# 72 direct columns in bf16 parts instead of 48 in f32, their sums added later, and comparisons that start later in a group

## The chip, the core and the metric

The kernel runs on one core of a Trainium2 chip. The core has a matmul engine (PE; its weight loads are listed as PEld), a vector engine (DVE), a scalar engine (ACT), a general engine (POOL) and a queue that issues transfers (SP). Each works through its own instructions in order, and they wait for one another by semaphores. The metric is device time in microseconds (us), the median of several executions; lower is better. A profile is one further execution, taken with the hardware profiler.

## What is computed

A graph layer on N = 6250 nodes and E = 206250 edges, 128 features each, all in f32:

```
edge_aggr = zeros(N, 128).at[src].add(edge_attr)
combined  = concat([x, edge_aggr, global_feat repeated], -1) @ W_c + b_c
h = softplus(combined @ W1 + b1)
h = softplus(h @ W2 + b2)
out = layernorm(x + h @ W3 + b3)
```

The edges are sorted by the other end (`dst`), so `src`, by which rows of `edge_attr` are summed, is in no order. This sum, over 206250 rows of 512 bytes, is nearly all of the work.

## The kernel before

**Edges as columns.** Edge e of the first 206208 lies on partition e // 1611 and in column e % 1611; the last 42 make one more column. A column is thus 128 edges, one on each partition. The 1612 columns are dealt with in two ways.

**Direct columns.** The first 48 are summed straight into the table of node sums, `sums_t` (features on partitions, 25 blocks of 256 nodes along the free axis). The nodes are cut into 13 windows of 512 (`WIDE`; the last holds 256). For a column and a window ACT makes a 128x512 table of ones and zeros, `hot`: one operation gives |node - position|, a second, over the two columns of a `QUAD` at once, gives max(0, 1 - that). PE multiplies the column's 128 rows (stationary, 128x128) with it and adds over the 12 columns of a `SET` in one PSUM tile, `direct_sum`, of which there are two. DVE then adds the tile to `sums_t`. The function `direct_steps` makes these steps: `begin` (node numbers, and for all windows the difference `less` that ACT uses as bias), `load` of the first set's rows, and one step per job (set, window, two columns). In step i ACT compares for job i (`compare`) and PE multiplies for job i - 2 (`add`). Where the sixth job of a window is done, the same `add` has DVE do the addition (L598). `hot` has three buffers, a set's rows two.

**Scattered columns.** The other 1564 are cut into 11 groups, given by `GROUPS` as (columns, sub). Within a group the rows are sorted by block of 256 nodes: `positions` counts and scans (DVE, PE) to find each edge's place. SP loads ten columns at a time (`load_rows`), POOL writes each row's code (`code_rows`, L639) and then sends each column's 128 rows to their places in one of three DRAM areas by an indirect DMA (`scatter_rows`, L647). `fill_rows` has set the area's unused places to -1 before. `reduce_steps` takes the group back in chunk loads of 1024 rows in block order: `load` (SP), `match` (L428, DVE: is the row's code equal to the position?, 128x2048; or the same by two kinds of ACT operations, L423 and L425), `product` (L442, PE, 16 instructions a load) and `add` (L459, DVE, one 128x256 addition per run of one block into `sums_t` at an offset read at run time). There are five chunk buffers, three of `hot` and three of the PSUM tile `part`.

**Which engine compares.** `TAIL` names, for the last groups, a share: every share-th chunk load is compared on DVE, the others on ACT. With (2, 4, 4) the last three groups have ACT on 1/2, 3/4 and 3/4 of their loads; all earlier groups are on DVE alone.

**The order.** The order of PE, DVE, ACT and SP is the order of the Python code. The main loop goes through the groups g, and in each through its tens of columns. Each ten loads rows three tens ahead (`LEAD`), scatters its own, and then issues a share of four lists: `prep` (positions of the next group), `sums` (the reduction of group g - 1, spread so that it ends at 95% of the group), `other` (node rows for the layers behind, in groups 3 to 5) and `filled`. To these come direct steps, spread over groups 1 to 6 in proportion to `left`, an estimate of each group's spare columns. The shares of one ten are interleaved evenly. `sums` begins with three chunk loads; of a group of 24 tens the first ten issues two steps, the second two more.

All transfers of SP are issued in one fixed order (`put_dma`), so a row load stands behind every chunk load ahead of it. After the last group its reduction is done alone, and the dense layers follow, in node tiles of 512.

Of the kernel before, what the change touches and what calls it, by code (L numbers as in the profile page):

```python
# [7 lines left out]
F32 = mybir.dt.float32  # L8
# [8 lines left out]
P = 128  # L17
# [5 lines left out]
GROUPS = ((40, 1), (120, 2), (200, 4), (240, 4), (240, 4), (240, 4), (226, 4), (130, 2), (72, 2),  # L23
# [4 lines left out]
TAIL = (2, 4, 4)  # L28
# [3 lines left out]
DIRECT = 48  # L32
SET = 12
WIDE = 512
QUAD = 2
FILL = 4
# [15 lines left out]
def kernel(  # L52
# [119 lines left out]
    with ExitStack() as phase:  # L172
# [377 lines left out]
        def direct_steps():  # L550


            steps = []
# [3 lines left out]
            less = keep.tile([P, NW, ND], F32, name="less")  # L557
            rows_in, hot_of, sum_of = {}, {}, {}

            def begin():  # L560

                first = keep.tile([P, NW], F32, name="first")
                nc.gpsimd.iota(first, pattern=[[WIDE, NW]], base=0, channel_multiplier=0,
                               allow_small_or_imprecise_dtypes=True)
                part, node, _ = whole_nodes(0, ND)
                nc.vector.tensor_copy(node, part)
                nc.vector.tensor_tensor(
                    less, node.unsqueeze(1).to_broadcast([P, NW, ND]),
                    first.unsqueeze(2).to_broadcast([P, NW, ND]), op=ALU.subtract)
# [6 lines left out]

            def compare(c, w, q):
                n = min(WIDE, NB * BL - w * WIDE)
                hot = direct_p.tile([P, QUAD, WIDE], F32, name="direct_hot", bufs=3)
                hot_of[c, w, q] = hot  # L580
                for j in range(QUAD):
                    nc.scalar.activation(hot[:, j, :n], iota_f[:, :n], AF.Abs,  # L582
                                         bias=less[:, w, c + q + j:c + q + j + 1], scale=-1.0)
                nc.scalar.activation(hot[:, :, :n], hot[:, :, :n], AF.Relu, bias=ones[:, :1],  # L584
                                     scale=-1.0)

            def add(c, w, q):
                n = min(WIDE, NB * BL - w * WIDE)
                k = min(SET, ND - c)
                hot = hot_of.pop((c, w, q))  # L590
                if q == 0:
                    sum_of[c, w] = ps.tile([P, WIDE], F32, name="direct_sum", bufs=2)
                for j in range(QUAD):
                    nc.tensor.matmul(sum_of[c, w][:, :n], rows_in[c][:, q + j, :], hot[:, j, :n],  # L594
                                     start=(q + j == 0), stop=(q + j == k - 1))
                if q + QUAD == k:
                    here = sums_t[:, w * WIDE:w * WIDE + n]
                    nc.vector.tensor_add(here, here, sum_of.pop((c, w))[:, :n])  # L598
# [3 lines left out]
            steps += [begin, lambda: load(0)]  # L602
            for i in range(len(jobs) + 2):
                def one(i=i):
                    if i < len(jobs):
                        c, w, q = jobs[i]
                        if (w, q) == (NW // 2, 0) and c + SET < ND:
                            load(c + SET)
                        compare(*jobs[i])
                    if i > 1:  # L610
                        add(*jobs[i - 2])
                steps.append(one)
# [42 lines left out]
        with tc.manual_schedule(engines={ET.PE, ET.DVE, ET.Activation, ET.SP}):  # L655
# [36 lines left out]
            for g in range(1, G - 4):  # L692
                left[g] = max(0.0, groups[g][1] - groups[g][0]
                              - groups[g - 1][3] * groups[g - 1][2] / 3 - (9 if 3 <= g < 6 else 0))
            direct_at = 0.0
# [3 lines left out]
            for g in range(G):  # L699
# [13 lines left out]
                for q in mine:  # L713
                    load_rows(i + LEAD)
# [5 lines left out]
                    for w, todo in enumerate((prep, sums, other, filled)):  # L720
                        share = (q - mine[0] + 1) / len(mine)
                        if w == 2:
# [182 lines left out]
```

## Time and profile before

| | us |
|---|---|
| median of 14 runs (2926.16 to 2974.1) | 2953.72 |
| profiled execution, its time | 2927.22 |
| its span, first to last instruction | 2925.3 |
| busy: PE, DVE, ACT, POOL | 1933.8, 1353.3, 891.4, 1588.0 |
| mean granted PE clock, as a share | 0.821 |

The scatters of the eleven groups begin at 26, 84, 266, 637, 1057, 1486, 1897, 2300, 2529, 2673 and 2739 us, and the last ends at 2778. What follows is the end of the reduction, to about 2850, and the layers.

In the profile a line such as L428 is a line of the kernel's file. A group is all instructions of one line, engine and operation: how many, their busy time, the mean of one in ns, the idle time of the engine just before them and what ended most of it. The ends of matmuls are modelled: of matmuls in a row the distance between starts tells the rate, not the duration. "Remote", or "another core or an unknown queue", is a wait whose end the profile can't put down to an instruction. The chain is the work that ended last, followed back from the end; only work on it, or work that would come onto it, moves the time.

### The profile page before, as it was taken

The page shows a single profiled execution, that of the slowest core. Times are in us where ns is not written, and L with a number is a line of the kernel's source. Part 1 is how long each engine was busy: PE and PEld are TensorE (multiplying, and loading weights), DVE is VectorE, ACT ScalarE, POOL GpSimd, SP SyncE. Part 2 cuts the span into 40 slices and gives each one's busy share as a digit, 9 for nine tenths or more (in the row PEclk, how much of TensorE's full clock was granted, in tenths as well). Part 3 has the DMA queues.
Part 4 walks back from the last instruction along what each step waited for, and adds up shares of the span by engine and source line. Part 5 has one row for each costly group of instructions (what it writes and reads, how often), then busy time and mean ns, then how long its engine had stood idle before and what let it go on. Part 6 is the DMA issues. An engine that isn't in the chain of part 4 may idle for free.

```text
span 2925.3 us, 21792 instructions
## 1 busy us (share of the span) xinstructions
PE 1933.8 (66%) x6470; PEld 1266.8 (43%) x6470; DVE 1353.3 (46%) x1976; ACT 891.4 (30%) x1186; POOL 1588.0 (54%) x1782
## 2 busy tenths in 40 slices
PE   2326387645887855768756777727877658747786
PEld 0113134422454532545433554524555446635663
DVE  5224344511544423554424554416554347647576
ACT  0223273423532413333214223204323200000586
POOL 5756446465456555555564655564555645554406
PEclk7557698776988977889878988868988879878898
DMA  9959347553454642556453445533545446645632
GB/s 286 260 156 253 92 135 212 154 160 93 136 175 148 182 131 82 152 139 174 132 155 95 142 131 155 146 93 104 156 133 154 139 123 195 187 118 158 169 88 88
DMA packets 418892, 437.18 MB, mean 149 GB/s; under 512 B 37807, under 2 KB 308774, under 8 KB 418774
## 3 DMA queue, kind: packets, MB, share of 16 engines
q1 hardware_dynamic: 368582, 332.43, 41.6%
q0 software_dynamic: 50048, 103.35, 10.8%
q8 instruction: 51, 0.84, 0.1%
q14 instruction: 67, 0.55, 0.1%
q10 hardware_dynamic: 144, 0.02, 0.0%
HBM read 262.62 MB, written 173.03 MB: 149 GB/s over the span
## 4 chain that ended last, share of the span: by engine, by line
PE 39%; another core or an unknown queue 28%; DVE 16%; issue 11%; ACT 4%; DVEq 1%; DMA 0%; ACTq 0%
PE part L442 26%; PE direct_sum L594 11%; DVE hot L428 5%; DVE sums_t L459 4%; ACT direct_hot L582 2%; DVE so_far L320 1%; ACT direct_hot L584 1%; DVE pos L354 1%; DVE sums_t L598 1%; DVE at L352 1%; DVE ib L266 1%; DVEq L453 1%; PE small L343 0%; ACT hot L423 0%
## 5 line engine op out<-in xcount | busy, mean ns | idle before, releaser
L647 POOL DMA_INDIRECT place<-rows,pos x1564 | 1505.6, 963 | 1231.0 <-DMA rows<-in_edge_attr 576.8
L442 PE MATMUL part<-hot,chunks 128*128 128x256 f32 x4524 | 1196.3, 421 | 667.0 <-DVE hot L428 342.1
L442 PEld LDWEIGHTS part<-hot,chunks 128*128 128x128 f32 x4524 | 941.1, 212 | 952.1 <-DVE hot L428 394.6
L582 ACT ACTIVATE direct_hot<-iota_f,less 128x512 f32<-128x512 f32 (+1 forms) x624 | 405.1, 696 | 1615.6 <-remote 703.5
L594 PE MATMUL direct_sum<-direct_hot,direct_rows 128*128 128x512 f32 (+1 forms) x1248 | 601.2, 612 | 135.1 <-ACT direct_hot L584 68.1
L428 DVE SCALAR_TENSOR_TENSOR hot<-chunks,iota_ps 128x2048 f32<-128x2048 f32 (+1 forms) x266 | 602.8, 2267 | 0.0
L459 DVE TENSOR_TENSOR sums_t<-sums_t,part 128x256 f32 x808 | 338.8, 419 | 462.8 <-remote 321.4
L594 PEld LDWEIGHTS direct_sum<-direct_hot,direct_rows 128*128 128x128 f32 x1248 | 244.0, 200 | 365.9 <-issue 267.1
L584 ACT ACTIVATE direct_hot<-direct_hot,ones 128x1024 f32<-128x1024 f32 (+1 forms) x312 | 348.6, 1117 | 10.2
L598 DVE TENSOR_TENSOR sums_t<-sums_t,direct_sum 128x512 f32<-128x512 f32 (+1 forms) x52 | 34.7, 667 | 628.9 <-remote 285.8
L423 ACT ACTIVATE hot<-iota_f,chunks 128x256 f32<-128x256 f32 x146 | 60.4, 497 | 374.8 <-PE part L442 357.8
L352 DVE TENSOR_TENSOR at<-small,ib 128x500 f32<-128x500 f32 (+3 forms) x80 | 52.9, 662 | 91.3 <-remote 71.6
L354 DVE TENSOR_REDUCE pos<-at 128x20 int32<-128x500 f32 (+3 forms) x80 | 86.9, 1086 | 2.7
L320 DVE TENSOR_TENSOR_SCAN so_far<-iota_ps,ib 128x1500 bf16<-128x1500 f32 (+7 forms) x30 | 85.9, 2863 | 0.0
L338 PE MATMUL small<-ib,upto_h 128*128 128x500 bf16 (+3 forms) x80 | 33.3, 417 | 67.5 <-DVE at L352 42.3
L533 DVE COPY x_t<-small 128x512 f32<-128x512 f32 (+1 forms) x13 | 8.6, 658 | 148.2 <-remote 115.8
L853 POOL TENSOR_TENSOR x_sb<-x_sb,b_all 128x512 f32<-128x512 f32 (+1 forms) x13 | 15.3, 1220 | 78.7 <-DMA x_sb<-in_x 78.7
L541 DVE TENSOR_SCALAR z_x<-small,z_bias 128x512 f32<-128x512 f32 (+1 forms) x13 | 9.3, 718 | 87.3 <-remote 39.9
L339 PE MATMUL small<-so_far,ones_h 128*128 128x500 bf16 (+3 forms) x80 | 33.7, 421 | 21.9 <-issue 11.4
L339 PEld LDWEIGHTS <-ones_h 128*128 128x128 bf16 x80 | 8.2, 103 | 90.4 <-issue 89.0
L266 DVE TENSOR_TENSOR ib<-block,iota_ps 128x1500 bf16<-128x1500 bf16 (+7 forms) x30 | 44.3, 1505 | 0.0
L277 PE MATMUL small<-ib,ones_h 128*128 128x500 bf16 (+3 forms) x80 | 24.2, 412 | 29.4 <-DVE ib L266 16.3
(117 smaller groups left out, 533.3 us busy)
## 6 DMA issues: line engine op xcount, KB each, us to landing
chunks<-place SPq DMA_DIRECT2D x281, 516.0 KB
rows<-in_edge_attr SPq DMA_DIRECT2D x154, 640.0 KB
place<-fill SPq DMA_DIRECT2D x252, 258.0 KB
place<-rows,pos POOLq DMA_INDIRECT x1564
x_sb<-in_x SPq DMA_DIRECT2D x24, 256.0 KB
direct_rows<-in_edge_attr SPq DMA_DIRECT2D x4, 768.0 KB
out<-y SPq DMA_DIRECT2D x12, 256.0 KB
src_i<-in_src SPq DMA_DIRECT2D x1, 761.5 KB
```

The lines of the kernel that those rows point to most:

```text
L266: nc.vector.tensor_tensor(ib, block[:, a:b].unsqueeze(1).to_broadcast([P, NB, n]), iota_ps[:, :NB].unsqueeze(2).to_broadcast([P, NB, n]), ...
L320: nc.vector.tensor_tensor_scan(t, iota_ps[:, 1:2].to_broadcast([P, NB * n]), in_block[k][0], 0.0, op0=ALU.mult, op1=ALU.add)
L352: nc.vector.tensor_mul(at, got.pop((k, j0)), in_block[k][1][:, :, j0:j1])
L354: nc.vector.tensor_reduce(pos[:, a - c0 + j0:a - c0 + j1], at.rearrange("p b g -> p g b"), axis=mybir.AxisListType.X, op=ALU.add)
L428: nc.vector.scalar_tensor_tensor(hot[:, :m], chunks[i][:, :m, D:W].to_broadcast([P, m, BL]), code_of(g), iota_ps.unsqueeze(1).to_broadcast ...
L442: nc.tensor.matmul(part[:, s - q, :], t[:, s * sub + j, :D], hot[:, s * sub + j], start=(j == 0), stop=(j == sub - 1))
L459: nc.vector.tensor_add(here, here, part[:, s - q, :])
L582: nc.scalar.activation(hot[:, j, :n], iota_f[:, :n], AF.Abs, bias=less[:, w, c + q + j:c + q + j + 1], scale=-1.0)
L584: nc.scalar.activation(hot[:, :, :n], hot[:, :, :n], AF.Relu, bias=ones[:, :1], scale=-1.0)
L594: nc.tensor.matmul(sum_of[c, w][:, :n], rows_in[c][:, q + j, :], hot[:, j, :n], start=(q + j == 0), stop=(q + j == k - 1))
L598: nc.vector.tensor_add(here, here, sum_of.pop((c, w))[:, :n])
L647: s = nc.gpsimd.indirect_dma_start(out=dst, out_offset=bass.IndirectOffsetOnAxis(ap=at, axis=0), in_=rows[:r, j, :], in_offset=None)
```

## The change

- `DIRECT` goes from 48 to 72, and the seventh entry of `GROUPS` from 226 to 202 columns: 24 columns move from the scattered to the direct ones. The direct sets go from four to six.
- The direct product is made in bf16. A new step, `split`, cuts each set's f32 rows on DVE into three bf16 parts that add up to the f32 value: the upper half of its bits, the upper half of what is left (written back into the lower half of the row's own place), and the rest (`direct_low`). PE multiplies each of the three with `hot`, now bf16, and adds them in the same f32 PSUM tile. `less` is made per set instead of once.
- The addition of a finished window to `sums_t` moves out of `add` into `total`, which is issued three steps later, at the head of a step.
- The first direct step is now the load of the first rows, and is issued in the last ten of group 0.
- In groups of more than eight tens the first ten issues the first three steps of `sums` (the chunk loads), and the later tens' shares are counted from the second ten on.
- `TAIL` has a fourth entry and other shares: group 7 and group 8 have ACT on half of their loads, the last two groups on all. `iota_f` grows to four blocks with it.

```diff
-GROUPS = ((40, 1), (120, 2), (200, 4), (240, 4), (240, 4), (240, 4), (226, 4), (130, 2), (72, 2),
+GROUPS = ((40, 1), (120, 2), (200, 4), (240, 4), (240, 4), (240, 4), (202, 4), (130, 2), (72, 2),
           (38, 1), (18, 1))
-TAIL = (2, 4, 4)
+TAIL = (2, 2, 100, 100)
-DIRECT = 48
+DIRECT = 72
+SPLIT = 2
...
-            less = keep.tile([P, NW, ND], F32, name="less")
-            rows_in, hot_of, sum_of = {}, {}, {}
+            node_f = keep.tile([P, ND], F32, name="node_f")
+            first = keep.tile([P, NW], F32, name="first")
+            less_of = {}
+            rows_in, low_in, hot_of, sum_of = {}, {}, {}, {}
...
+            def halves(t):
+                return [t.bitcast(BF16).rearrange("p c (d h) -> p c d h", h=2)[:, :, :, h]
+                        for h in (0, 1)]
+            def split(c):
+                n = min(SET, ND - c)
+                less = less_of[c] = direct_p.tile([P, NW, SET], F32, name="less", bufs=2)
+                nc.vector.tensor_tensor(
+                    less[:, :, :n], node_f[:, c:c + n].unsqueeze(1).to_broadcast([P, NW, n]),
+                    first.unsqueeze(2).to_broadcast([P, NW, n]), op=ALU.subtract)
+                low_in[c] = direct_p.tile([P, SET, D], BF16, name="direct_low", bufs=2)
+                for a in range(0, min(SET, ND - c), SPLIT):
+                    b = min(a + SPLIT, SET, ND - c)
+                    rest = direct_p.tile([P, SPLIT, D], F32, name="direct_rest")[:, :b - a]
+                    x_c = rows_in[c][:, a:b]
+                    nc.vector.tensor_sub(rest, x_c, halves(x_c)[1])
+                    nc.vector.tensor_sub(low_in[c][:, a:b], rest, halves(rest)[1])
+                    nc.vector.tensor_copy(halves(x_c)[0], halves(rest)[1])
...
-                hot = direct_p.tile([P, QUAD, WIDE], F32, name="direct_hot", bufs=3)
+                hot = direct_p.tile([P, QUAD, WIDE], BF16, name="direct_hot", bufs=3)
...
-                for j in range(QUAD):
-                    nc.tensor.matmul(sum_of[c, w][:, :n], rows_in[c][:, q + j, :], hot[:, j, :n],
-                                     start=(q + j == 0), stop=(q + j == k - 1))
+                for j in range(q, q + QUAD):
+                    addends = halves(rows_in[c][:, j:j + 1]) + [low_in[c][:, j:j + 1]]
+                    for i, part in enumerate(addends):
+                        nc.tensor.matmul(sum_of[c, w][:, :n], part[:, 0], hot[:, j - q, :n],
+                                         start=(j == 0 and i == 0), stop=(j == k - 1 and i == 2))
                 if q + QUAD == k:
-                    here = sums_t[:, w * WIDE:w * WIDE + n]
-                    nc.vector.tensor_add(here, here, sum_of.pop((c, w))[:, :n])
+                    ready.append((c, w, n))
+            def total():
+                c, w, n = ready.pop(0)
+                here = sums_t[:, w * WIDE:w * WIDE + n]
+                nc.vector.tensor_add(here, here, sum_of.pop((c, w))[:, :n])
...
-            steps += [begin, lambda: load(0)]
-            for i in range(len(jobs) + 2):
+            steps += [lambda: load(0), begin, lambda: split(0)]
+            ready, behind = [], []
+            for i in range(len(jobs) + 6):
                 def one(i=i):
+                    if behind and behind[0] <= i:
+                        behind.pop(0)
+                        total()
                     if i < len(jobs):
                         c, w, q = jobs[i]
                         if (w, q) == (NW // 2, 0) and c + SET < ND:
                             load(c + SET)
+                        if (w, q) == (NW - 2, 0) and c + SET < ND:
+                            split(c + SET)
                         compare(*jobs[i])
-                    if i > 1:
+                    if 1 < i < len(jobs) + 2:
                         add(*jobs[i - 2])
+                        if len(ready) > len(behind):
+                            behind.append(i + 3)
...
+            direct_first = direct[:1]
+            direct = direct[1:]
...
+                    if g == 0 and q == mine[-1]:
+                        for step in direct_first:
+                            step()
                     load_rows(i + LEAD)
...
                         share = (q - mine[0] + 1) / len(mine)
+                        if w == 1 and len(mine) > 8:
+                            if q == mine[0]:
+                                now.append(todo[:3])
+                                done[w] = 3
+                                continue
+                            share = (q - mine[0]) / (len(mine) - 1)
```

More of the change, by code (lines that the diff above doesn't have):

```diff
@@ L556, in direct_steps @@
             NW = -(-NB * BL // WIDE)
-            less = keep.tile([P, NW, ND], F32, name="less")
-            rows_in, hot_of, sum_of = {}, {}, {}
+            node_f = keep.tile([P, ND], F32, name="node_f")
+            first = keep.tile([P, NW], F32, name="first")
+            less_of = {}
+            rows_in, low_in, hot_of, sum_of = {}, {}, {}, {}
             def begin():
-                first = keep.tile([P, NW], F32, name="first")
                 nc.gpsimd.iota(first, pattern=[[WIDE, NW]], base=0, channel_multiplier=0,
                                allow_small_or_imprecise_dtypes=True)
[L565 to L569, printed above, removed]
+                part, _, _ = whole_nodes(0, ND)
+                nc.vector.tensor_copy(node_f, part)
             def load(c):
@@ L582, in compare @@
                     nc.scalar.activation(hot[:, j, :n], iota_f[:, :n], AF.Abs,
-                                         bias=less[:, w, c + q + j:c + q + j + 1], scale=-1.0)
+                                         bias=less_of[c][:, w, q + j:q + j + 1], scale=-1.0)
                 nc.scalar.activation(hot[:, :, :n], hot[:, :, :n], AF.Relu, bias=ones[:, :1],
```

## The prediction

> **What bounds the kernel now.** I read the busy shares first (PE 66%, POOL 54%, DVE 46%, ACT 30%: nothing is full), then the chain that ended last, the groups, the stretches of single groups, and the timeline where the chain waits. The chain, by engine and by line:
>
> ```profile
> PE 39%; another core or an unknown queue 28%; DVE 16%; issue 11%; ACT 4%; DVEq 1%; DMA 0%; ACTq 0%
> PE part L442 26%; PE direct_sum L594 11%; DVE hot L428 5%; DVE sums_t L459 4%; ACT direct_hot L582 2%; DVE so_far L320 1%; ACT direct_hot L584 1%; DVE pos L354 1%; DVE sums_t L598 1%; DVE at L352 1%; DVE ib L266 1%; DVEq L453 1%; PE small L343 0%; ACT hot L423 0%
> ```
>
> POOL, whose 1564 scatters are the largest group, is not on it. The groups of lines (busy time, mean of one, idle time before and what ended it) say why:
>
> ```profile
> L647 POOL DMA_INDIRECT place<-rows,pos x1564 | 1505.6, 963 | 1231.0 <-DMA rows<-in_edge_attr 576.8
> L582 ACT ACTIVATE direct_hot<-iota_f,less 128x512 f32<-128x512 f32 (+1 forms) x624 | 405.1, 696 | 1615.6 <-remote 703.5
> L594 PE MATMUL direct_sum<-direct_hot,direct_rows 128*128 128x512 f32 (+1 forms) x1248 | 601.2, 612 | 135.1 <-ACT direct_hot L584 68.1
> L584 ACT ACTIVATE direct_hot<-direct_hot,ones 128x1024 f32<-128x1024 f32 (+1 forms) x312 | 348.6, 1117 | 10.2
> L598 DVE TENSOR_TENSOR sums_t<-sums_t,direct_sum 128x512 f32<-128x512 f32 (+1 forms) x52 | 34.7, 667 | 628.9 <-remote 285.8
> ```
>
> POOL stands 577 us for rows that SP has not yet asked for: SP issues rows and chunks in one order, and stands for chunk buffers that PE must free. So PE with DVE and ACT sets the pace. Two stretches (second and fourth group's scatters; columns PE, PEld, DVE, ACT, POOL busy, granted clock):
>
> ```profile
> 265.70:636.70 371.00, 230.94 (x683) 129.69 (x682) 148.30 (x213) 154.83 (x198) 196.25 (x220) 0.82 0.56 155
> 1057.30:1486.20 428.90, 298.26 (x975) 197.26 (x974) 183.15 (x214) 126.07 (x156) 235.95 (x265) 0.82 0.47 135
> ```
>
> In the later one PE is busy 298 of 429 us, POOL's 240 scatters at 1.27 us would take 304. The rest is waiting. Two kinds stand in the timeline. First, work of PE that is over by its record is seen by others much later, while POOL scatters without a gap:
>
> ```profile
> 1919.07 0.60 PE L531 MATMUL small<-ident,x_sb 128*128 128x128 f32 x4
> 1936.56 0.96 POOL L647 DMA_INDIRECT place<-rows,pos  x1 [0.30 <-issue]
> 1964.44 0.69 DVE L533 COPY x_t<-small 128x512 f32<-128x512 f32 x1 [51.60 <-remote]
> ```
>
> There is one core, so "another core or an unknown queue" is this kind. Second, DVE stands in `direct_steps`' addition (L598) for a matmul issued in the same step, comes late to the next comparison (L428), and PE stands for that:
>
> ```profile
> 2174.54 1.88 PE L594 MATMUL direct_sum<-direct_hot,direct_rows 128*128 128x512 f32 x4
> 2176.26 0.93 PE L277 MATMUL small<-ib,ones_h 128*128 128x500 bf16 x4
> 2176.46 0.69 DVE L598 TENSOR_TENSOR sums_t<-sums_t,direct_sum 128x512 f32<-128x512 f32 x1 [9.47 <-PE direct_sum L594]
> 2177.06 2.28 DVE L428 SCALAR_TENSOR_TENSOR hot<-chunks,iota_ps 128x2048 f32<-128x2048 f32 x1
> 2179.40 3.72 PE L442 MATMUL part<-hot,chunks 128*128 128x256 f32 x16 [2.21 <-DVE hot L428]
> ```
>
> **The change, part by part**, against the profiled execution (2927.2 us, span 2925.3); the runs' median is 0.9% above it.
>
> *Direct matmuls.* One f32 product is two instructions (1248 for 48 columns x 26 halves of 13 windows). Four of 512 elements start within 1.88-0.59 = 1.29 us: 0.43 each. Of four bf16 ones of 500 the first starts at 2176.26, the third at 2176.69: 0.215 each. Before: 1152 x 0.43 + 96 narrow x 0.215 = 516 us. After: 72 x 3 products in 12 wide windows and a narrow one, 2592 x 0.215 + 216 x 0.11 = 581. That is +65, and at the granted 0.82 +79. On the path all of it, or 11% of the span out of 601 us busy (0.53), which gives 42: between them **+60**. The weight loads (103 ns for contiguous bf16 in the by-shape groups, 190 for f32) are shorter than a matmul, strided halves included unless they exceed f32's.
>
> *Direct comparisons.* 312 pairs become 468: 754 us of ACT become 1131, +377. The `hot` tile in bf16 has no row here; nearest is the same operation in f32, so no gain is taken. The Trainium skill, "ScalarE: Activation LUTs", section "What ACT_TABLE_LOAD costs", says one element a cycle for f32 and bf16 alike, which speaks against hoping for more; by it the term stays as it is, while at twice the speed it would be 565 us of ACT and -22 here. No run here shows a bf16 one yet. On the path: 3% of the span out of 754 us (0.12), **+44**. Ends: 0 where ACT stays hidden; 137 where the first two groups go by ACT. The schedule puts 66 and 97 pairs on their 12 and 20 tens of columns (43 and 63 before): 5.5 x 2.41 = 13.3 us per ten against 12.7 of scattering. 57 added pairs x 2.41 = 137.
>
> *Splitting on DVE.* Per two columns two subtractions and a copy of 256 elements; nearest rows of 240 take 0.41, 0.41, 0.28. 36 x 1.10 = 40, six smaller `less` against one of 0.81, +1; 26 more additions, +17. 58 us, of which DVE's share on the chain (468 of 1353, 0.35) gives **+20**; ends 0 and 58. Each split is 19 operations, about 7 us in one piece; behind it stand the comparisons, and PE for them. Its own reader comes 12 pairs later. In the trace a two-input subtraction-like row (L203, 0.41 us, at 737.74) stands beside scatters at 737.39 and 738.65, 1.26 apart as always. The Trainium skill, "SBUF — State Buffer", section "Who interferes with whom", would have such an operation shut out a GpSimd one that reads SBUF; by that rule POOL would lose up to 40 us, by the row nothing, and the row is taken.
>
> *Later additions.* `total` runs three steps after the last matmul, so DVE no longer drains PE. What goes is the pause behind it, 0.69 + 2.28 less what PE still holds; 2.21 is seen, 52 x 2.2 = 114. What is late next is L459, which lets DVE lead PE by two chunk loads only, and in the "unknown" waits needs the same late news of PE. So **-80**; ends 0 and -171 (half of the 342 us, 236.0 and 106.2, that the waits of L598 show for PE and issue rather than "remote").
>
> *24 columns fewer to scatter.* 24 x 1.27 = 30 us of POOL, not on the chain. Reduction: L442, L428 and L459 have 35% of the span, 1024/1564 x 24 = 16; the unknown waits scale with scatters, 819/1564 x 24 = 13. **-29**; ends -10, -46 (both and POOL's own).
>
> *The last groups' comparisons.* ACT alone for the last two. A pure ACT load takes 3.30 + 2.00 less overlap = 5.24 us; from 2784 to 2849 the 14 loads took 4.6 each: +9. Half of group 7's 23 comparisons leave DVE (4.1 us a load with additions) for a stage paced by PE's 3.5: -7 at best, little under its waits. **+8**; ends -7, +16.
>
> *Group starts.* The code sets `done` to 3 and then back: in groups 1 to 6 the second ten's share rounds to 1 or 2 of the steps. So nothing is compared there, one or two loads are issued a second time (8 in all; the instruction list of SP has 290 chunk loads, 282 wanted), and comparisons begin with the third ten in groups of 24 tens, not the second (with the second in group 7 alone). On SP three chunk loads, which wait for the last group's scatters, now stand together ahead of the next rows; each repeat takes one of five chunk buffers and 516 KB. Direct work fills the time. **+6**; ends -40 (DVE no longer stands for the first chunk) and +40 (8 x 5 us). The first `direct_rows` load moves ahead of two row loads on SP, before the first group's end: 0, three tens of rows are already there; ends -15 (the wait it had) and +3.
>
> Sum: 60 + 44 + 20 - 80 - 29 + 8 + 6 = **+29**, 2956; times 2953.72/2927.22 = 1.009: **2983 us**, 1% slower.
>
> **Rivals.** *The additions give more* (faster). For it: 629 us of DVE standing, PE's 342 us for comparisons. Against: 286 of the 629 are "remote", which a deferral by 7 us does not outlast. At -171 the sum is -62: 2865, times 1.009 **2891**. It decides once PE's wait for L428 falls by more than 125 us.
> *ACT becomes the bound early.* For it 13.3 against 12.7 us, and ACT's 703 us of late news. Against: those stretches took 15.2 and 18.6 us per ten anyway. With 137 for 44: 3049, **3077**.
> *It cancels*: additions near -110; 2926, **2953**.
> *The change does not do what it says*: the start of the comparisons is shifted by another ten and repeats loads, as worked out; alone +-40, within the cases above.
>
> **How the numbers follow.** Forecast (slower by 0.5 to 2.5%) 0.38, additions 0.34, ACT 0.15, cancelling 0.13; so slower 0.53, same 0.13, faster 0.34. 0.5%, 15 us, is about what a measurement of this kernel can tell from no change. Distances to the ends, added as squares, make 124 us; 8 in 10 about 100 either side: **2885 to 3080**. The forecast's own range is 2968 to 3028.
>
> **What would show it.** L594's successor: 2808 matmuls, 0.215 apart at full clock, near 600 us of work. ACT direct near 1130 us, its bf16 form at 0.71. The addition's idle time far below 629, PE's wait for comparisons below 342 by some 80. Scatter waits for rows about as before: if they fall by over 100 us, the rival of the additions holds. If the stretch of the first two groups grows by 100, ACT's does. 290 chunk loads. I am wrong if the "unknown" 28% moves by itself: I scale it by scatters, yet nothing in the trace says what starts it.

## The result, and the profile after

The changed kernel takes 3057.35 us (median of 10 runs, 3030.7 to 3072.44) against 2957.06 us before: a ratio of 1.0356, 95% interval 1.0322 to 1.039. It is slower by 3.6%, where I had forecast 1%. The ratio, here and below, is that of the fast runs of both kernels alone and so can lie a little off the quotient of the medians, here 1.034. The chain that ended last, by engine and by line, after the change:

```profile
PE 41%; another core or an unknown queue 26%; ACT 16%; issue 12%; DVE 5%; DVEq 0%; ACTq 0%
PE part L444 26%; PE direct_sum L620 12%; ACT direct_hot L606 7%; ACT direct_hot L608 6%; DVE hot L430 2%; ACT hot L425 1%; DVE sums_t L461 1%; PE small L345 1%; PE small L340 0%; PE small L341 0%; PE small L342 0%; ACT away L828 0%; ACT away L823 0%; ACT away L822 0%
```

DVE has largely left the chain (16% to 5%) and ACT has come onto it (4% to 16%); PE grew by 2 points of a longer span, and the unknown part stayed at 0.8 ms. The groups (busy, mean of one in ns, idle time before and what ended most of it); L687, L606, L608, L620 and L628 are what L647, L582, L584, L594 and L598 were, and L444, L430 and L461 are L442, L428 and L459:

```profile
L687 POOL DMA_INDIRECT place<-rows,pos x1540 | 1478.9, 960 | 1382.6 <-DMA rows<-in_edge_attr 705.6
...
L606 ACT ACTIVATE direct_hot<-iota_f,less 128x512 bf16<-128x512 f32 (+1 forms) x936 | 604.8, 693 | 1375.5 <-remote 965.3
...
L620 PE MATMUL direct_sum<-direct_hot,direct_rows 128*128 128x512 bf16 (+1 forms) x1872 | 598.6, 402 | 443.2 <-issue 242.8
...
L608 ACT ACTIVATE direct_hot<-direct_hot,ones 128x1024 bf16<-128x1024 bf16 (+1 forms) x468 | 521.9, 1115 | 15.2
...
L628 DVE TENSOR_TENSOR sums_t<-sums_t,direct_sum 128x512 f32<-128x512 f32 (+1 forms) x78 | 51.9, 666 | 371.0 <-remote 197.8
```

The addition's idle time fell from 629 to 371 us, but ACT now stands 965 us for "remote" (703 before) and POOL 706 us for rows (577). The stages of the scatters of groups 2 and 4, counted from 0 (the same two, with the same columns, as in the prediction):

```profile
285.40:701.50 416.10, 267.19 (x1074) 142.45 (x1073) 167.77 (x259) 252.69 (x322) 195.84 (x220) 0.82 0.50 141
1148.80:1611.00 462.20, 319.30 (x1277) 199.46 (x1278) 197.65 (x245) 202.21 (x256) 235.53 (x264) 0.84 0.44 128
```

They were 371 and 429 us long. The scatters of groups 1 to 7 now begin at 84, 285, 702, 1149, 1611, 2061 and 2434 us. So groups 1 to 5, which hold most of the direct work, are 164 us longer, and group 6 is 30 us shorter, for its 24 columns fewer; the span grew by 127. In none of these stages is an engine full. The timeline of the changed kernel (start, duration) shows the standing. Here ACT waits to write a table again whose last reader on PE was over at 797 us, and starts at 807, 3 us after POOL went idle. I call this a late count: PE's work is over, and the engine that waits for it is told later.

```profile
796.77 0.42 PE L620 MATMUL direct_sum<-direct_hot,direct_low 128*128 128x256 bf16 x1
...
803.31 0.96 POOL L687 DMA_INDIRECT place<-rows,pos  x1 [0.30 <-issue]
804.27 0.21 POOL L679 COPY rows<-src_i 128x10 f32<-128x10 f32 x1
...
807.33 0.91 ACT L606 ACTIVATE direct_hot<-iota_f,less 128x256 bf16<-128x256 f32 x2 [11.63 <-remote]
...
809.04 0.59 PE L620 MATMUL direct_sum<-direct_hot,direct_rows 128*128 128x256 bf16 x2 [11.85 <-ACT direct_hot L608]
```

### The profile page after: what moved, and what is told of

It is laid out like the page before. It is cut to its first block, busy times and chain, and to the rows that moved or that the text cites. A ratio compares the mean times of both kernels' runs of the same rounds, so it can differ in the third digit from the quotient of the medians.

```text
span 3052.0 us, 25528 instructions
## 1 busy us (share of the span) xinstructions
PE 2008.2 (66%) x7977; PEld 1277.0 (42%) x7977; DVE 1367.9 (45%) x2089; ACT 1322.9 (43%) x1781; POOL 1560.5 (51%) x1756
## 4 chain that ended last, share of the span: by engine, by line
PE 41%; another core or an unknown queue 26%; ACT 16%; issue 12%; DVE 5%; DVEq 0%; ACTq 0%
PE part L444 26%; PE direct_sum L620 12%; ACT direct_hot L606 7%; ACT direct_hot L608 6%; DVE hot L430 2%; ACT hot L425 1%; DVE sums_t L461 1%; PE small L345 1%; PE small L340 0%; PE small L341 0%; PE small L342 0%; ACT away L828 0%; ACT away L823 0%; ACT away L822 0%
## 5 line engine op out<-in xcount | busy, mean ns | idle before, releaser
L687 POOL DMA_INDIRECT place<-rows,pos x1540 | 1478.9, 960 | 1382.6 <-DMA rows<-in_edge_attr 705.6
L444 PE MATMUL part<-hot,chunks 128*128 128x256 f32 x4476 | 1151.1, 411 | 379.7 <-issue 230.4
L606 ACT ACTIVATE direct_hot<-iota_f,less 128x512 bf16<-128x512 f32 (+1 forms) x936 | 604.8, 693 | 1375.5 <-remote 965.3
L444 PEld LDWEIGHTS part<-hot,chunks 128*128 128x128 f32 x4476 | 908.7, 206 | 606.3 <-issue 293.5
L620 PE MATMUL direct_sum<-direct_hot,direct_rows 128*128 128x512 bf16 (+1 forms) x1872 | 598.6, 402 | 443.2 <-issue 242.8
L461 DVE TENSOR_TENSOR sums_t<-sums_t,part 128x256 f32 x802 | 336.4, 419 | 689.2 <-remote 475.1
L430 DVE SCALAR_TENSOR_TENSOR hot<-chunks,iota_ps 128x2048 f32<-128x2048 f32 x248 | 563.7, 2275 | 0.0
L608 ACT ACTIVATE direct_hot<-direct_hot,ones 128x1024 bf16<-128x1024 bf16 (+1 forms) x468 | 521.9, 1115 | 15.2
L620 PEld LDWEIGHTS <-direct_rows 128*128 128x128 bf16 x1872 | 189.3, 103 | 702.2 <-issue 539.8
L620 PE MATMUL direct_sum<-direct_hot,direct_low 128*128 128x512 bf16 (+1 forms) x936 | 376.0, 402 | 39.1 <-issue 38.6
L628 DVE TENSOR_TENSOR sums_t<-sums_t,direct_sum 128x512 f32<-128x512 f32 (+1 forms) x78 | 51.9, 666 | 371.0 <-remote 197.8
L620 PEld LDWEIGHTS <-direct_low 128*128 128x128 bf16 x936 | 97.1, 104 | 163.6 <-issue 76.0
L356 DVE TENSOR_REDUCE pos<-at 128x20 int32<-128x500 f32 (+2 forms) x79 | 85.6, 1083 | 2.7
L354 DVE TENSOR_TENSOR at<-small,ib 128x500 f32<-128x500 f32 (+2 forms) x79 | 52.2, 660 | 65.0 <-remote 30.0
L427 ACT ACTIVATE hot<-hot,ones 128x2048 f32<-128x2048 f32 (+2 forms) x34 | 65.1, 1914 | 1.1
```

The source lines that it names most:

```text
L354: nc.vector.tensor_mul(at, got.pop((k, j0)), in_block[k][1][:, :, j0:j1])
L356: nc.vector.tensor_reduce(pos[:, a - c0 + j0:a - c0 + j1], at.rearrange("p b g -> p g b"), axis=mybir.AxisListType.X, op=ALU.add)
L427: nc.scalar.activation(hot[:, :m], hot[:, :m], AF.Relu, bias=ones[:, :1], scale=-1.0)
L430: nc.vector.scalar_tensor_tensor(hot[:, :m], chunks[i][:, :m, D:W].to_broadcast([P, m, BL]), code_of(g), iota_ps.unsqueeze(1).to_broadcast ...
L444: nc.tensor.matmul(part[:, s - q, :], t[:, s * sub + j, :D], hot[:, s * sub + j], start=(j == 0), stop=(j == sub - 1))
L461: nc.vector.tensor_add(here, here, part[:, s - q, :])
```

## The experiments

### On a chip where the effect is absent

The first four runs fell on a chip on which the kernel before took 2163.33 us, not 2957. They take the change apart: 48 columns instead of 72; the later additions alone, put into the kernel before; the old starts and last groups; and ACT's second operation left out, so that the sums of the direct columns are wrong.

```diff
-GROUPS = ((40, 1), (120, 2), (200, 4), (240, 4), (240, 4), (240, 4), (202, 4), (130, 2), (72, 2),
+GROUPS = ((40, 1), (120, 2), (200, 4), (240, 4), (240, 4), (240, 4), (226, 4), (130, 2), (72, 2),
...
-DIRECT = 72
+DIRECT = 48
```

> The change with 48 direct columns in place of 72 (groups as before: 226 columns in group 6); bf16 product, later additions, shifted starts and last groups stay. After took 3057 us, before 2957. Theory A (ScalarE's comparisons set the length of groups 1 to 5: 15.6 us of ScalarE a column, 376 us for 24 columns): with the old number of columns ScalarE has the slack that it had before, the freed VectorE counts, and the time falls below before, to 2890 to 2940 us. Rival B (TensorE's three bf16 products for one float32 product are too dear): of 2808 bf16 matmuls 1872 stay, so two thirds of the loss stay: 3010 to 3040 us. Rival C (the repeated loads and later starts of the groups cost the 100 us): 3040 to 3085 us, since 24 more scattered columns come on top.

```diff
-                    here = sums_t[:, w * WIDE:w * WIDE + n]
-                    nc.vector.tensor_add(here, here, sum_of.pop((c, w))[:, :n])
+                    ready.append((c, w, n))
...
+                    if behind and behind[0] <= i:
+                        behind.pop(0)
+                        total()
...
+                        if len(ready) > len(behind):
+                            behind.append(i + 3)
```

> The kernel before with nothing but the later additions (float32 product, 48 direct columns, old starts). Before took 2957 us. My forecast's term: the additions' wait gives -80 us, so 2875 to 2885 us, at most -171. Theory A (ScalarE takes VectorE's place on the chain as soon as VectorE is free): at 48 columns ScalarE is busy 754 us directly and had idle time, so most of the gain should show: 2870 to 2910 us. Rival D (the additions' idle time was only the place where TensorE's late counts were seen, and the next reader waits for the same): 2940 to 2965 us.

```diff
-TAIL = (2, 2, 100, 100)
+TAIL = (2, 4, 4)
...
-                        if w == 1 and len(mine) > 8:
-                            if q == mine[0]:
-                                now.append(todo[:3])
-                                done[w] = 3
-                                continue
-                            share = (q - mine[0]) / (len(mine) - 1)
```

> The change with the old starts of the groups (comparisons from the first ten columns on, no chunk loaded twice) and the old comparisons of the last groups; 72 bf16 columns and later additions stay. After took 3057 us. Theory A (ScalarE's comparisons of the direct columns): 3040 to 3070 us, for only the 8 repeated loads and some idle time at the starts go. Rival C (starts and repeated loads are the cause): 2950 to 3000 us.

```diff
-                nc.scalar.activation(hot[:, :, :n], hot[:, :, :n], AF.Relu, bias=ones[:, :1],
-                                     scale=-1.0)
```

> The change without the second ScalarE operation of each direct comparison (ReLU of one minus the distance): the tables hold the distances themselves, so the sums of the 72 direct columns are not the reference's. ScalarE loses 468 instructions of 1.115 us, 522 us; TensorE and VectorE keep all they had. After took 3057 us. Theory A (ScalarE is the bound of groups 1 to 5): the time falls by 100 us and more, to 2860 to 2960 us, and ScalarE's share of the chain goes from 16% to under 6%. Rival B (TensorE's added matmuls are the bound): 3030 to 3060 us.

Measured, as ratios to the kernel before on that chip: 48 columns 1.0009 (1.0 to 1.0019), later additions 1.0006 (0.9997 to 1.0016), old starts 0.988 (0.9864 to 0.9897), no second operation 0.988 (0.9864 to 0.9897). No expectation fits, since none had this machine in mind. Only the number of scattered columns counts among these edits: 24 fewer give 25 us. The chain of the version with 48 columns has no unknown part, and POOL's scatters and their transfers lead; its group of scatters follows:

```profile
DMA 25%; PE 24%; POOL 23%; issue 12%; DVE 10%; ACT 4%; SPq 1%; DVEq 1%; POOLq 0%; ACTq 0%
```

```profile
L687 POOL DMA_INDIRECT place<-rows,pos x1564 | 1502.6, 961 | 481.2 <-issue 413.5
```

A scatter costs POOL the same 961 ns as before, but POOL hardly stands for rows (9 us in all). The 800 us between the two chips are about the size of the unknown part, 28% of 2925 us, which suggests that they are that part and what follows from it; these runs alone do not show it, since the granted clock differs too (0.92 to 0.95 in these four profiles, 0.82 in before).

### The same runs where before takes 2960 us

> The changed kernel itself, beside the kernel before on one chip. The first four experiments ran on a chip on which the kernel before took 2163 us, not 2957, and its page has none of the 28% of the chain put down to another core or an unknown queue. There GpSimd's scatters set the pace (73% busy in every slice), and 24 scattered columns fewer gave -25 us whatever else was changed. Theory A (the loss of 100 us exists only where TensorE's counts are seen late): where the kernel before takes about 2163 us, the changed one takes 2130 to 2142 us, a gain of 1.2%; where before takes about 2957 us, 3030 to 3075 us. Rival (the shifted starts, the one part that is in no run so far with all others, cost time on any chip): 2150 to 2200 us where before takes 2163 us.

> The change with 48 direct columns, again. Where before takes about 2163 us: 2160 to 2168 us, as in the first run. Where before takes about 2957 us, the numbers of its first expectation are still to be told apart: 2890 to 2940 us if ScalarE's comparisons of the 24 added columns make the loss, 3010 to 3040 us if the bf16 products do, 3040 to 3085 us if the starts do.

> The kernel before with the later additions alone, again. Where before takes about 2163 us: 2160 to 2168 us. Where before takes about 2957 us: 2870 to 2910 us if the freed VectorE counts, as my forecast took it (-80 us); 2940 to 2965 us if the next reader waits for the same late counts of TensorE.

> The change without the second ScalarE operation, again (the tables hold distances, so the sums of the direct columns are not the reference's). Where before takes about 2163 us: 2134 to 2140 us. Where before takes about 2957 us: 2860 to 2960 us if ScalarE sets the length of groups 1 to 5, 3030 to 3060 us if TensorE's added matmuls do.

Before took 2960.45 us here. The change: 3056.62, ratio 1.0359 (1.0283 to 1.0436), as in the result. With 48 columns 2959.9, 1.0005 (0.9958 to 1.0052). Later additions alone 2919.36, 0.9884 (0.98 to 0.9969). Without ACT's second operation 3011.73, 1.019 (1.0103 to 1.0277).

So the 24 columns cost all of the 97 us, and the rest cancels: the additions give 1.2%, and something takes it back. ACT's 522 us less give 1.7%, half of the loss; theory A had asked for 100 us, and rival B, which had asked for at most 27, fails as well. Where the columns' time goes is seen on POOL's line, with 48 columns on the same kind of chip:

```profile
L687 POOL DMA_INDIRECT place<-rows,pos x1564 | 1501.8, 960 | 1277.9 <-DMA rows<-in_edge_attr 585.6
```

With 72 columns it stood 1382.6 us in the profile shown above, 105 more; its waits for rows alone grew by 120 (on this chip 1383.6 us, and by 191). POOL saves 23 us of scatters and stands 105 us longer while PE and ACT do direct work.

### Starts, product, and fewer columns

The old starts and last groups again, then the same with 48 columns (both edits as above), two products of three, and fewer columns.

> The change with the old starts of the groups and the old comparisons of the last groups, again (72 bf16 columns and later additions stay). Where before takes about 2960 us: the changed kernel took 3057, 96 us more; with 48 columns it took 2960, so the 24 columns cost those 96; and the later additions alone gave -41, so bf16 product, splitting, starts and last groups together must cost 41 at 48 columns. Theory C2 (the starts with their repeated loads, and the last groups, cost that 41): 3005 to 3025 us. Rival S (it is the splitting and the bf16 product): 3045 to 3065 us. Where before takes about 2163 us: 2138 us, as in the first run.

> 48 direct columns, bf16 product, later additions, old starts and old last groups: against the later additions alone (2919 us where before takes 2960) it differs by the product and its splitting only. TensorE's direct work is 502 us in place of 629 (both measured where before takes 2960), so by TensorE's share of the chain it should be faster: 2870 to 2910 us (theory C2: starts and last groups cost the 41 us, and the cheaper product is a gain). Rival S (the splitting on VectorE, some 40 us, and the smaller steps cost as much as the product saves, and the starts cost nothing): 2945 to 2965 us. Where before takes about 2163 us: 2160 to 2168 us.

```diff
-                    addends = halves(rows_in[c][:, j:j + 1]) + [low_in[c][:, j:j + 1]]
+                    addends = halves(rows_in[c][:, j:j + 1])
...
-                         start=(j == 0 and i == 0), stop=(j == k - 1 and i == 2))
+                         start=(j == 0 and i == 0), stop=(j == k - 1 and i == 1))
```

> The change without the third product of each direct column: the lowest part of every number is still split off on VectorE but not added, so the sums of the 72 direct columns keep some 16 bits of each number. TensorE loses 936 matmuls, a third of 729 us, 243 us; ScalarE and VectorE keep all. Where before takes about 2960 us and the change 3057: theory P (24 more columns cost what they take of TensorE, at its share of the chain, 41%): 2940 to 2980 us. Rival A (ScalarE's comparisons hold the path; leaving out their second operation gave -45 us): 3030 to 3060 us. Where before takes about 2163 us: 2130 to 2140 us.

The same with 36 columns (the seventh group then has 238):

```diff
-GROUPS = ((40, 1), (120, 2), (200, 4), (240, 4), (240, 4), (240, 4), (226, 4), (130, 2), (72, 2),
+GROUPS = ((40, 1), (120, 2), (200, 4), (240, 4), (240, 4), (240, 4), (238, 4), (130, 2), (72, 2),
...
-DIRECT = 48
+DIRECT = 36
```

> As with 48 direct columns, bf16 product, later additions and old starts, but 36 columns. Where before takes about 2960 us: 24 columns cost 97 us, 4.0 us each, so 12 columns fewer should give -48 us against the version with 48, if each column costs the same (theory: TensorE and ScalarE together set the pace, and a direct column costs more there than its scatter costs GpSimd). Rival: under 48 columns GpSimd's scatters and the late counts, which grow with the scattered columns, take over, and the time stays within 10 us of the version with 48. Where before takes about 2163 us, GpSimd is the bound and 12 more scattered columns cost 12 times 1.27 us: 2173 to 2180 us.

A third chip; before took 2984.77 us. Old starts: 3090.72, 1.0376 (1.0329 to 1.0424). The starts, the repeated loads and the last groups cost nothing that can be measured (1.0376 here, 1.0359 with the new ones on the second chip; the intervals overlap); C2 falls. 48 columns with old starts: 2995.93, 1.0046 (1.0007 to 1.0084), so the bf16 product with its splitting is 1.6% slower than the float32 product of the later additions alone (0.9884, from another chip; on one chip, 1.0005 against 0.9884, it is 1.2%, starts included; each figure is good to about a point either way), though PE's direct work is 127 us less (629 and 502 us). Two products instead of three: 3049.05, 1.0237 (1.0184 to 1.0289): a third of PE's direct work, 243 us by count, gives some 40 us, and theory P falls. The profile has 526 us of direct work for 729, 203 less, but 92 of its 1872 matmuls are missing there. 36 columns: 2948.08, 0.9876 (0.9815 to 0.9936), 48 us below 48 columns: 4.0 us a column, as expected.

The waits of PE's instructions that no event explains (total, times, longest) say where the product's gain went. First the later additions alone in float32, then 48 columns in bf16 with old starts:

```profile
PE part L442 <- issue: 336.8, 172, 30.5
PE direct_sum L594 <- issue: 83.3, 41, 15.8
```

```profile
PE part L444 <- issue: 345.1, 249, 8.9
PE direct_sum L620 <- issue: 152.4, 79, 13.4
```

420 us became 498; in before it was 318, in the changed kernel 512, and on the first chip, with the later additions, 0.7. A part of these may be waits whose event is missing in the profile, so I counted in the traces the idle time above 0.25 us ahead of PE instructions (matmuls and weight loads) that wait for no semaphore: 73 us in before, 161 with the later additions, 296 in bf16 with 48 columns, 0 in all four runs of the first chip. PE itself stands, not only its readers.

The chunk products, which no edit touched, became longer as well, here in the later additions alone and in 48 columns in bf16, both on one chip:

```profile
L442 PE MATMUL part<-hot,chunks 128*128 128x256 f32 x4524 | 1186.0, 415 | 581.2 <-issue 336.8
```

```profile
L444 PE MATMUL part<-hot,chunks 128*128 128x256 f32 x4524 | 1224.3, 423 | 576.2 <-issue 299.2
```

The granted clock was 0.828 in the first and 0.797 in the second (0.782 with old starts on the third chip). With two products of three it was 0.793 for 0.818, and the chunk products took 1192 us for 1151. So of the 127 us that PE's direct work lost, 38 came back in the chunk products and some 78 in standing. Why the clock fell was not tested.

### What starts the late counts

In the trace of before I took every pause of POOL over 1.5 us that began while a count of PE was late by over 1.5 us. Counted from the end of POOL's last scatter there are 37; in 35 of them the count came within 6.5 us, in 21 within 3. A stop is not the only end of such a wait: of ACT's 49 of over 5 us in before, 22 ended within 6 us after a stop. And it does not show which follows which, so I gave POOL pauses: an operation of its own that changes nothing, on the ten rows about to be scattered.

```diff
             nc.gpsimd.tensor_copy(rows_at[i][:r, :k, D:W], low[:r, c:c + k].unsqueeze(2))
+            wait = rows_at[i][:r, :k, :D]
+            nc.gpsimd.tensor_scalar(wait, wait, 1.0, None, op0=ALU.mult)
```

> The kernel before with one GpSimd operation more for each ten columns, a multiplication of the ten rows' 1280 numbers a partition by one, so that GpSimd issues no scatter for some 2 to 3 us. In the trace of before, 35 of the 37 late counts of TensorE that were open when GpSimd stopped arrived within 6.5 us of its stop, most within 3. Theory L (uninterrupted scatters hold the counts back): 156 pauses of 2 to 3 us cost at most 310 to 470 us of GpSimd, the 1029 us of late counts shrink below 500, and the time falls from about 2960 to 2550 to 2800 us; the 28% 'unknown' of the chain falls below 12%. Rival (the counts are late for a reason outside GpSimd, and GpSimd's stops only follow): 2960 to 3150 us, the 'unknown' share unchanged. Where before takes about 2163 us: 2450 to 2650 us, GpSimd being the bound.

> The changed kernel with the same pauses. Theory L: with fewer late counts the added direct work lies beside the scatters again, and the order of the two kernels turns: 1 to 2% below the kernel before with pauses, since 24 columns fewer are scattered and 2 pauses fewer made. Rival (the 24 columns cost what TensorE and ScalarE need for them, late counts or not): 70 to 110 us above the kernel before with pauses.

> The later additions alone (float32, 48 columns) with the same pauses. Theory L: within 1% of the kernel before with pauses, as on the chip without late counts, where they made no difference. Rival (VectorE's standing for the additions costs time in itself): 1.5% and more below it.

A fourth chip; before took 2971.04 us. Before with pauses: 2702.41, 0.9111 (0.9033 to 0.9188). The change with pauses: 2662.42, 0.8981 (0.8903 to 0.9059). Later additions with pauses: 2702.5, 0.9109 (0.9031 to 0.9187). The times and the unknown part are as theory L has them in each: 3.4 us more work on POOL for every ten columns makes the kernel 9% faster, and the order of the two kernels turns: the change is 1.5% faster (2662 against 2702). Before with pauses: the chain, the groups of scatters and pauses, and ACT's wait that was the longest (total, times, longest):

```profile
POOL 60%; issue 18%; PE 9%; DVE 6%; DMA 3%; another core or an unknown queue 2%; ACT 1%; DVEq 0%; SPq 0%; POOLq 0%; ACTq 0%
```

```profile
L649 POOL DMA_INDIRECT place<-rows,pos x1564 | 1510.1, 966 | 477.6 <-issue 423.1
...
L641 POOL TENSOR_SCALAR rows<-rows 128x1280 f32<-128x1280 f32 x159 | 541.6, 3408 | 1.5 <-DMA rows<-in_edge_attr 0.8
```

```profile
ACT direct_hot L582 <- remote: 169.9, 18, 19.7
```

The unknown part goes from 28% to 2%, and POOL, at 79% busy, no longer stands for rows (0.8 us). It leads the chain now, and the change has 24 columns fewer for it to scatter. ACT's "remote" goes from 703.5 to 169.9 us, but that label is not clean, since its "issue" waits rise from 191 to 445. One number of the expectation misses: counts are late for 878 us in all (1029 in before), not under 500. That tally goes by the recorded events, and these are incomplete: of 825 counts of PE the profile has 704 in before and 644 here (all on the first chip), and a missing one passes for late until the next. ACT itself tells it without them. Its idle time after the last matmul that reads the table's old contents was over, added over all direct jobs, is 768 us in before and 164 here (27 and 7 such waits of over 10 us), 994 in the changed kernel, and at most 1 in the four runs of the first chip. In the other direction nothing is late: where nothing else holds it, PE starts on ACT's table within 1.3 us, in before, here and in the changed kernel.

> 48 direct columns, bf16 product, later additions, old starts, without the splitting: no subtraction and no copy on VectorE, and all three products take the high half of each number, so the sums of the direct columns are not the reference's. TensorE and ScalarE keep all. Against the version with splitting (1.0046 of before) and the later additions alone in float32 (0.988 of before). If the splitting is what costs: 0.975 to 0.99 of before. If the bf16 product itself gives nothing, for instance because it only shortens what TensorE does while its counts are late: 1.00 to 1.01.

```diff
-                    nc.vector.tensor_sub(rest, x_c, halves(x_c)[1])
-                    nc.vector.tensor_sub(low_in[c][:, a:b], rest, halves(rest)[1])
-                    nc.vector.tensor_copy(halves(x_c)[0], halves(rest)[1])
...
-                    addends = halves(rows_in[c][:, j:j + 1]) + [low_in[c][:, j:j + 1]]
+                    addends = [halves(rows_in[c][:, j:j + 1])[1]] * 3
```

Measured: 2993.11, 1.012 (1.001 to 1.0229). Splitting is not what costs: the result is a little above the range in which the bf16 product itself gives nothing, and far from the other. The sums of the direct columns are wrong here, since all three products take the same part.

### How long a pause

```diff
-            wait = rows_at[i][:r, :k, :D]
+            wait = rows_at[i][:r, :k, :D // 2]
```

> The changed kernel with pauses of half the numbers (640 a partition, some 1.7 us) after each ten columns. With full pauses it took 2662 us and GpSimd was the bound: 1945 us of scatters at their pace, 533 of pauses, 184 behind the last scatter. If a pause of 1.7 us is enough for the late counts to arrive: 2395 to 2450 us, GpSimd still the bound. If the counts need the 2 to 3 us that most of them took after a stop in the trace of before: 2550 to 2900 us, with the 'unknown' part back in the chain.

```diff
-            wait = rows_at[i][:r, :k, :D]
-            nc.gpsimd.tensor_scalar(wait, wait, 1.0, None, op0=ALU.mult)
+            if i % 2:
+                wait = rows_at[i][:r, :k, :D]
+                nc.gpsimd.tensor_scalar(wait, wait, 1.0, None, op0=ALU.mult)
```

> The changed kernel with full pauses (3.4 us) after every second ten columns only; the same 270 us of GpSimd as with half pauses after each ten. If the length of a pause decides and a dense run of 25 us between pauses can be bridged by the buffers (three tables of direct comparisons, five chunks): 2395 to 2500 us. If the frequency decides, since TensorE's readers stand up to 25 us until the next pause: 2600 to 2800 us.

The chip is the fourth again; before took 2949.02 us. Half pauses: 2454.45, 0.8349 (0.8278 to 0.842), 4 us above the range, and POOL is not the bound that I expected it to be. Full pauses every twenty columns: 2820.77, 0.9598 (0.947 to 0.9726). For the same time of POOL (283 and 266 us) the frequency decides, and more than I expected: the second is above its range. ACT's idle time behind late counts, as above, is 396 us with half pauses and 711 with pauses every twenty. Half pauses, the chain and the group of pauses:

```profile
PE 40%; ACT 15%; POOL 15%; issue 12%; DVE 9%; another core or an unknown queue 8%; DMA 1%; DVEq 1%; ACTq 0%; SPq 0%; POOLq 0%
```

```profile
L681 POOL TENSOR_SCALAR rows<-rows 128x640 f32<-128x640 f32 (+2 forms) x157 | 282.8, 1803 | 29.0 <-DMA rows<-in_edge_attr 28.3
```

1.8 us for every ten columns are enough for most of it, PE, ACT and POOL share the chain, and the granted clock is 0.916, where the change without pauses has 0.818. This version beats both kernels: 16.5% less than before and, by the ratios 0.8349 and 1.0356, some 19% less than the change. On a chip like the first it was not tried; there POOL is the bound, and 283 us of pauses would be added to about 2138, an estimate of 2420 against 2163.

## Why the prediction was wrong

The direction and the range (2885 to 3080) held; the size was off by more than a factor of three. That the direction held is partly luck: the sum hides larger errors of opposite sign. By the prediction's own rows, its +60 for matmuls splits into -119 for making 48 columns in bf16 and +179 for 24 columns more (work of 387 against 516 us, and 194 more, times 60/65).

| step | forecast, us | measured |
|---|---|---|
| bf16 product and splitting, 48 columns | -119 + 13 | +36 to +48 (1.2 to 1.6%, about 1% either way) |
| 24 columns more: PE, ACT, splitting, scatters | 179 + 44 + 7 - 29 | +95 and +97 |
| later additions | -80 | -34 (-59 to -9) |
| starts, last groups | +14 | none |
| whole change | +29 | +100 |

*Direct matmuls: the step that failed.* "11% of the span out of 601 us busy (0.53)", or all of it, turned busy time into time on the path. The work was nearly right: 728.6 us busy after against 601.2, +127 where I had 65 warm and 79 at the granted clock. But on chips with late counts a microsecond of PE's direct work is not worth a fixed share. Taking a third of it away gave some 40 us (0.16 of the 243 by count), and 127 us less at 48 columns gave nothing: PE stood longer without a cause that the profile shows (498 us for 420), and its chunk products took 38 us more at a lower granted clock, which I had held at 0.82. I counted on a gain of 119 that is not there. What makes PE stand stays open.

*Direct comparisons.* Right in its rows: L606 and L608 take 693 and 1115 ns in bf16 (696 and 1117 in f32), 1127 us in all for 1131. The Trainium skill, "ScalarE: Activation LUTs", section "What ACT_TABLE_LOAD costs", has one element a cycle for both types, and the trace agrees that the type makes no difference. The price was near too: 522 us of ACT removed gave 1.7%, 0.09 to 0.1 per us for my 0.12. The stretches of groups 1 and 2 grew by 65 us, short of the 100 by which the rival of ACT was to be known.

*24 columns.* 243 us of PE (the 24 columns take 226, from 502 to 729) and 522 us of ACT (they take 376), each removed alone, gave 40 and 45 to 50 us; scaled, 37 and 34 of the 97. The other 26 and the 29 that I credited for scatters are not assigned: removing both at once was not tried. That credit is real only on the first chip, with 25 us.

*Splitting.* No cost seen. The Trainium skill, "SBUF — State Buffer", section "Who interferes with whom", has a DVE instruction with two SBUF inputs contend with a GpSimd one that reads SBUF; it does not show in the scatters of any run here, which take 960 ns after and 963 before.

*Later additions.* The mechanism was right: their idle time went from 629 to 100 us in the version with nothing else changed (L602 there), and, as the prediction named it, L459 was late next, its "remote" waits rising from 321.4 to 581.0:

```profile
L459 DVE TENSOR_TENSOR sums_t<-sums_t,part 128x256 f32 x808 | 338.8, 419 | 818.8 <-remote 581.0
...
L602 DVE TENSOR_TENSOR sums_t<-sums_t,direct_sum 128x512 f32<-128x512 f32 (+1 forms) x52 | 34.5, 664 | 100.4 <-PE direct_sum L594 42.3
```

The size was half. The rival of the additions was to decide once PE's wait for comparisons fell by 125: it fell by 235 (342.1 to 107.2), and the kernel got slower, so that mark was wrong. The scatters' waits for rows did not fall, as it needed; they rose by 129.

*Group starts.* Within their bounds.

*The unknown part.* I scaled it by scatters and wrote that nothing in the trace says what starts it. The trace did: the lines that I quoted stop short of POOL's pauses, and all I drew from them was that POOL scattered. The runs speak against a tax per scatter: with as many scatters, pauses took it from 28% to 2%, and on the first chip it is absent. It is the state in which all other terms have their price: where it was ended, the change was 1.5% faster than the kernel before, and where it is absent 1.2% (with the old starts).

## What to carry to other kernels

A large "unknown" part of the chain is to be explained before anything is priced beside it: list where such waits end, and see what another engine did just then. While it stands, shares of the chain are no prices; a change is better tried with that state removed. And the engine that looks idle enough may be the one to slow down: here 283 us more work on POOL, well placed, made the changed kernel some 19% faster, by the ratios of two chips.

## What was not expected of the hardware

On three of the four chips of the experiments, PE's counts reached ACT up to some 50 us late (42.7 in before, 50.8 in the changed kernel) while POOL sent scatters 1.26 us apart or soon after it stopped, and PE stood 73 to 306 us ahead of instructions that wait for nothing. On the first chip neither occurred, and the kernel before took 2163 us. With pauses of POOL of 1.8 us for every ten columns, the waits of ACT of over 10 us fall from 45 to 3, and PE's standing from 187 to 33 us. For every twenty columns they are too seldom. Which part of the machine holds the counts back, what makes PE stand, and why one chip is free of both, stays open.

The granted clock of PE fell where its direct work was cut (0.828 to 0.797 with 48 columns in bf16) and rose where its counts were less late (0.916 with half pauses). What drives it was not tested.
